# A four-layer graph network on one core: where the last blocks' own parts stand at the end of layer 1

## The chip, the cores and the metric

The kernel runs on one core of a Trainium2 chip. A core has TensorE (PE, matrix products), VectorE (DVE), ScalarE (ACT), GpSimd (POOL) and SyncE (SP). Each engine works through its own instructions in the order written and waits on semaphores for the others. POOL issues the gathers, SP nearly all other transfers. The metric is the device time of one launch in microseconds; lower is better.

## The reference, cut to what matters

Four graph layers run in turn on 3327 nodes with 512 features, each followed by a residual and a layer norm, all with the same 0/1 matrix `adj`:

```python
x = layernorm(x + L0_gat(x, adj))                 # attention, 8 heads of 64
x = layernorm(x + L1_mean(x, adj))                # relu(combine(self, mean of neighbours))
x = layernorm(x + L2_first64(x, adj))             # below
x = layernorm(x + L3_gat(x, adj))                 # attention, 4 heads of 128

# layer 2
keep = (A > 0) & (cumsum(A > 0, axis=1) <= 64)    # the first 64 neighbours of a row
nb_mean = keep @ X / max(keep.sum(axis=1), 1)
xj = leaky_relu(nb_mean @ W_nb.T + b_nb)          # zero where a row has no neighbours
xi = leaky_relu(X @ W_line.T + b_line)            # a node's "own part"
out = xi + xj
```

## The kernel before, in words

The nodes are cut into 26 blocks of 128 (the last, block 25, has 127). Every row of `adj` is first turned into lists of neighbours. Layers 1 and 2 then work block by block: a block has some chunks of 128 list places, a chunk's table rows are gathered from DRAM by an indirect DMA of POOL (L1018, `gather`), and TensorE multiplies a 0/1 selection matrix with the gathered rows and adds up in PSUM (L1879, `mean_group`). Layer 2's neighbour product is applied ahead of the gathering: the table `t2_d` holds `X @ W_nb.T + b_nb` for every node, in three bfloat16 pieces. A neighbour can be any node, so no gather of layer 2 can be issued before all 26 blocks are stored in `t2_d`.

The instruction order is written out by generators. A generator issues some instructions and yields; `work` holds groups of chunks, `ends` the tails of blocks, and one `step` lets every live generator go on to its next `yield`, in the order in which they were added. What is issued first stands first in its engine's queue. `both()` steps `work` and then `ends`.

The blocks come in the order `weave`: 1, 24, 23, ..., 9, 8, 7, 6, 25. After a block's sum is done, `layer1_end(b)` goes through these stages, one for each step:

- the layer's result with residual (L1933 to L1935) and the statistics (L811, L813), and a square root on ScalarE (L819);
- a reciprocal and three small corrections on VectorE (L821, L834 to L836), and the normalised block `xres[b]` (L851);
- its transposition on TensorE (L789), evacuated by ScalarE to `xt` (L792);
- the product with `wn2` (L806);
- the bias added into `tb` (L1946), and then, over the following steps, the split of `tb` into three pieces `t3` (L842 to L848, ScalarE and VectorE in turn), and the store into `t2_d` (L777, SP);
- three small products `acc0 += near0 @ t3` (L1958), which sum block 0's neighbours without a gather. Once all 26 are in, `acc0` is evacuated and added to `xres[0]` (L1963 to L1966).

The own part of layer 2, `own_part(b)`, needs only the normalised block: a product with `wl2` (L806) from the same `xt`, then three VectorE operations (L1977 to L1979) that add the result to `xres[b]`. For most blocks it is added to `ends` beside the split. For the last five blocks of `weave` (`LATE = 5`: 9, 8, 7, 6 and 25) it is put off: the block goes onto the list `late`, and its own part later transposes the block again. Before the change, block 9's own part is added when the last groups of layer 1 are under way, and the own parts of 8, 7, 6 and 25 after layer 2's first two groups of gathers have been issued.

Layer 2's stage opens after that. Its loads of `first2`, `raw3` and `a3` (L2037, L2043, L2046) go into space that `wn2` and `wl2` leave, so they wait for the last product with `wl2`. `score_weights` (L1570 to L1573) prepares layer 3's weights on VectorE, and `layer2_end(b)` is the tail of a block of layer 2. The gathers go into a ring of 19 chunks (tiles `gl` and `gk`). `select` (L1034) makes a selection matrix on VectorE and keeps it in `salla`, and later `sallb`.

Of the kernel before, what the change touches and what calls it, by code (L numbers as in the profile page):

```python
# [631 lines left out]
def sparse_path(ctx, tc, flag_i, x, adj, l0_w, l0_a1, l0_a2, l1_w_self, l1_b_self, l1_w_nb, l1_b_nb,  # L632
# [15 lines left out]
    NB = (N + P - 1) // P  # L648
# [7 lines left out]
    def row(src, n, rows=P):  # L656
        return bass.AP(tensor=src.tensor, offset=src.offset, ap=[[0, rows], [1, n]])

    def pool_in(lay, name, bufs=1, **kw):
        return lay.enter_context(tc.tile_pool(name=name, bufs=bufs, reuse_waits="tile", **kw))  # L660
# [23 lines left out]
    def mixed():  # L684


        left, ahead = list(range(1, NB - 1)), 0
        mean = sum(chunks_of[1:]) / (NB - 1)
        while left:
            b = left.pop(0 if ahead >= 0 else -1)  # L690
            ahead += mean - chunks_of[b]
            yield b
        yield NB - 1

    weave = list(mixed())
# [79 lines left out]
    def store(dst_d, b, t, shift=0):  # L775
        for p0, p1 in rows_of(b):
            nc.sync.dma_start(dst_d[shift + b * P + p0:shift + b * P + p1, :], t[p0:p1])  # L777
# [7 lines left out]
    def transposed(pool, ps, src, xsum=None, b=0):  # L785

        pt = ps.tile([P, DC, P], F32, name="pt", tag="tr")
        for c in range(DC):
            nc.tensor.transpose(pt[:, c, :], src[:, c * P:(c + 1) * P], ident)  # L789
        xt = pool.tile([P, DC, P], F32, name="xt")  # L790
        if xsum is None:
            nc.scalar.copy(xt, pt)  # L792
            return xt
        n = LAST if b == NB - 1 else P
        for c in range(DC):
            nc.scalar.activation(xt[:, c, :n], pt[:, c, :n], AF.Identity, accum_out=xsum[:, c, b:b + 1])  # L796
        if n < P:
            xs = pool.tile([P, DC], F32, name="xs")
            nc.vector.tensor_reduce(xs, xsum, AX.X, ALU.add)
            nc.vector.tensor_scalar(xt[:, :, n], xs, 1.0 / N, None, ALU.mult)  # L800
        return xt

    def times(ps, xt, w):
        po = ps.tile([P, D], F32, name="po")
        for c in range(DC):
            nc.tensor.matmul(po, xt[:, c, :], w[:, c], start=c == 0, stop=c == DC - 1)  # L806
        return po

    def moments(fin, y):
        st = fin.tile([P, 6], F32, name="st")  # L810
        nc.vector.bn_stats(st, y)  # L811
        mv = fin.tile([P, 2], F32, name="mv")
        nc.vector.bn_aggr(mv, st)  # L813
        return mv

    def root(fin, mv):

        r0 = fin.tile([P, 1], F32, name="r0")
        nc.scalar.activation(r0, mv[:, 1:2], AF.Sqrt, bias=eps)  # L819
        yield  # L820
        nc.vector.reciprocal(r0, r0)  # L821
        return newton(fin, mv, r0)
# [27 lines left out]
    def scaled(o, y, mv, rs):  # L850
        nc.vector.tensor_scalar(o, y, mv[:, 0:1], rs, ALU.subtract, ALU.mult)  # L851
# [1033 lines left out]
    ends = Stages()  # L1885

    def both():
        work.step()
        ends.step()
# [9 lines left out]
    with ExitStack() as lay:  # L1899
        fin = pool_in(lay, "l1f", 2)  # L1900
        wp = pool_in(lay, "l2b")
        bn = wp.tile([P, D], F32, name="bn")
        nc.sync.dma_start(bn, row(l2_b_nb, D))
        bl = wp.tile([P, D], F32, name="bl")
        nc.sync.dma_start(bl, row(l2_b_line, D))
        sp = pool_in(lay, "l1s", 3)
        ps = pool_in(lay, "l1ps", 2, space=PSUM)
        acc0 = pool_in(lay, "l1p0", space=PSUM).tile([P, D], F32, name="acc0")
        paccz = pool_in(lay, "l1pz", space=PSUM)
        nd = [0]  # L1910
        xts = pool_in(lay, "l1xt", 3)
        first = extra[:, 4 * D:].rearrange("p (s d) -> p s d", s=2)
        nc.sync.dma_start(first.bitcast(F32), t1_d[2:2 + P, :])
        early, late = list(range(NB - LATE0, NB - LATE0 + EARLY)), []

        def self_part(b):

            yield
            xt = transposed(xts, ps, xres[b])
            yield  # L1920
            zb = xin.get(b)
            if zb is None:
                zb = fin.tile([P, D], F32, name="tb")
            nc.scalar.copy(zb, times(ps, xt, wx))
            if b in xin:
                return
            store(z1_d, b, zb)

        def layer1_end(b, acc):
            yield  # L1930
            zb = xin.pop(b)
            y = fin.tile([P, D], F32, name="e")
            nc.vector.scalar_tensor_tensor(y, acc, rdeg[:, b:b + 1], zb, ALU.mult, ALU.add)  # L1933
            nc.vector.tensor_add(y, y, bias1)
            nc.vector.scalar_tensor_tensor(y, y, 0.0, xres[b], ALU.max, ALU.add)  # L1935
            mv = moments(fin, y)
            rs = yield from root(fin, mv)
            x2 = xres[b]
            scaled(x2, y, mv, rs)
            yield  # L1940
            xt = transposed(xts, ps, x2)
            yield
            po = times(ps, xt, wn2)
            yield
            tb = fin.tile([P, D], F32, name="tb")
            nc.vector.tensor_add(tb, po, bn)  # L1946
            t3 = fin.tile([P, 3, D], BF16, name="t3")
            if b not in weave[-LATE:]:
                ends.add(own_part(b, xt))
            else:  # L1950
                late.append(b)
            yield from pieces(t3, tb)
            store(t2_d, b, t3.rearrange("p s d -> p (s d)"), 2)
            yield
            m = LAST if b == NB - 1 else P
            nd[0] += 1
            for k in range(3):
                nc.tensor.matmul(acc0, near0[:m, b, :], t3[:m, k], start=nd[0] == 1 and k == 0,  # L1958
                                 stop=nd[0] == NB and k == 2)
            if nd[0] == NB:  # L1960
                yield
                y = fin.tile([P, D], F32, name="e")
                nc.scalar.mul(y, acc0, rnear)  # L1963
                yield
                nc.vector.scalar_tensor_tensor(y, y, SAGE_ALPHA, y, ALU.mult, ALU.max)
                nc.vector.tensor_add(xres[0], y, xres[0])  # L1966

        def own_part(b, xt=None):

            yield  # L1970
            if xt is None:
                xt = transposed(xts, ps, xres[b])
                yield
            po = times(ps, xt, wl2)
            yield
            xi = fin.tile([P, D], F32, name="xi")
            nc.vector.tensor_add(xi, po, bl)  # L1977
            nc.vector.scalar_tensor_tensor(xi, xi, SAGE_ALPHA, xi, ALU.mult, ALU.max)
            nc.vector.tensor_add(xres[b], xi, xres[b])  # L1979

        def made(b):

            xin[b] = fin.tile([P, D], F32, name="zb", bufs=3)
            if b < NB - LATE0 + EARLY:
                load(xin[b], z1_d, b)
            else:
                ends.add(self_part(b))

        for b in early:
            ends.add(self_part(b))  # L1990
        ends.drain()
        for item in woven(ring):
            b, at = item[0], item[4]
            if at == 0 and b or b == 0 and at + item[3] == NB:
                made(b)
            work.add(mean_group(item, t1_d, row0, lambda b, acc: ends.add(layer1_end(b, acc)), [first]))
            both()
            if b in weave[-HASTE:]:
                ends.step()
        ends.add(own_part(late.pop(0)))  # L2000
        while work.live:
            both()
        ends.drain()
        wxlay.close()
        rows = room.tile([P, RING], F32, name="gl", tag="ring")
        extra = aside.tile([P, MORE], F32, name="gk", tag="aside")
        ring = Ring(3 * D, rows.bitcast(BF16), extra.bitcast(BF16))
        sall = [(0, pool_in(ctx, "s_alla", side="right").tile([P, split, P], FP8, name="salla"))]
        nexts = groups(ring, weave, first=(1, 2))

        def second(b, acc):
            ends.add(layer2_end(b, acc))

        firsts = []
        for _ in range(2):
            work.add(mean_group(next(nexts), t2_d, None, second, firsts, sall))
            work.step()
        for b in late:
            ends.add(own_part(b))
        while ends.live:  # L2020
            ends.step()
    w2lay.close()


# [191 lines left out]
```

## Time and profile before

| | |
|---|---|
| median of 3 runs | 1661.63 us (1660.79 to 1669.61) |
| profiled execution | 1659.49 us, its span 1657.7 us |
| PE busy | 1487.2 us, 90% of the span |
| DVE busy | 1175.7 us, 71% |
| ACT busy | 903.4 us, 54% |
| POOL busy | 762.6 us, 46% |
| last gather of layer 1 issued | 1046.69 us |
| first gather of layer 2 issued | 1099.08 us |
| mean granted TensorE clock | 0.955 |

The first row is what the kernel is judged by. All other numbers are of one profiled execution, whose positions are counted from the start of its span. A row of instructions names the engine, the line of the kernel, the operation, what it writes and reads, and in brackets how long its engine had been idle and what ended that. Lines such as L789 and L806 are helpers that many places call, so the tile names tell which call it is: `po<-wn,xt` is a product for the table, `po<-wl,xt` one for an own part. The trace writes `wn2` as `wn` and `t2_d` as `t_d`, without numbers. One `times` call shows as eight product records, one `transposed` as four.

### The profile page before, as it was taken

The numbers are of one execution on the slowest core, as the hardware profiler recorded it, in microseconds if no ns is written. First come the engines' busy times: TensorE is split into PE (matmuls) and PEld (weight loads), VectorE is DVE, ScalarE is ACT, GpSimd is POOL, SyncE is SP. The second block draws the span as 40 slices with busy tenths as digits, with TensorE's granted clock in tenths as the row PEclk, the third lists the DMA queues.
The fourth block names the chain that finished last, engine by engine and source line by source line (L and its number), as shares of the span: only waits on it lengthen the run. The fifth ranks groups of instructions, "written<-read, shape, count | busy, mean of one in ns | idle before, by whom it ended". The sixth has DMA issues, their size and how long they took to land.

```text
span 1657.7 us, 24457 instructions
## 1 busy us (share of the span) xinstructions
PE 1487.2 (90%) x7305; PEld 998.9 (60%) x7341; DVE 1175.7 (71%) x3136; ACT 903.4 (54%) x3007; POOL 762.6 (46%) x994
## 2 busy tenths in 40 slices
PE   6789968999999999889999999887999996988885
PEld 4567746666666777435555555433566665777764
DVE  7998789998567789215566677648665644779886
ACT  5788865777667878412222121212344444679997
POOL 3000057665554520055444565137777702777770
PEclk9889979999999999879999999999999999999998
DMA  8877678876665542199788999348899812888881
GB/s 253 267 240 263 194 254 280 269 214 207 204 192 152 169 140 81 52 367 317 246 298 312 326 371 337 132 143 296 297 322 295 285 52 91 241 240 249 255 248 64
DMA packets 130402, 381.99 MB, mean 230 GB/s; under 512 B 22037, under 2 KB 36477, under 8 KB 130259
## 3 DMA queue, kind: packets, MB, share of 16 engines
q0 software_dynamic: 67696, 252.97, 47.6%
q1 hardware_dynamic: 62563, 127.35, 22.8%
q8 instruction: 60, 0.98, 0.2%
q14 instruction: 83, 0.68, 0.1%
HBM read 331.89 MB, written 48.37 MB: 229 GB/s over the span
## 4 chain that ended last, share of the span: by engine, by line
PE 63%; DVE 11%; ACT 9%; DMA 8%; issue 5%; POOL 3%; SPq 0%; ACTq 0%; DVEq 0%; POOLq 0%
PE po L806 19%; PE acc L1375 12%; PE po L1056 10%; PE acc L1879 9%; PE pt L789 3%; DMA gl<-t_d,idx 3%; DMA gt<-t_d,idx 1%; PE acc L1871 1%; PE acc L1263 1%; DVE gt L1356 1%; PE acct L1485 1%; DVE cand L909 1%; ACT m L882 1%; ACT upc L1412 1%; POOL gl L1018 1%
## 5 line engine op out<-in xcount | busy, mean ns | idle before, releaser
L1018 POOL DMA_INDIRECT gt<-t_d,idx x201 | 203.8, 1014 | 342.3 <-DVE eq L978 208.0
L1018 POOL DMA_INDIRECT gl<-t_d,idx x265 | 269.6, 1017 | 134.8 <-DMA t_d<-t 51.4
L1375 PE MATMUL acc<-gt,sel 128*128 128x264 f32 (+3 forms) x804 | 209.9, 408 | 4.4 <-DVE gt L1356 2.7
L1018 POOL DMA_INDIRECT gm<-t_d,idx x140 | 140.4, 1003 | 143.9 <-PE acc L1879 95.6
L806 PE MATMUL po<-wn,xt 128*128 128x512 f32 x416 | 193.9, 608 | 7.1 <-ACT h L1526 3.8
L1375 PEld LDWEIGHTS acc<-gt,sel 128*128 128x128 f32 (+3 forms) x804 | 153.4, 200 | 42.0 <-issue 13.9
L1375 PE MATMUL acc<-gl,sel 128*128 128x260 f32 (+3 forms) x524 | 137.5, 410 | 11.0 <-ACT r L1553 4.9
L806 PEld LDWEIGHTS po<-wn,xt 128*128 128x128 f32 x416 | 77.8, 194 | 89.1 <-issue 76.2
L1056 PE MATMUL po<-gt,xt 128*128 128x268 f32 x416 | 118.1, 428 | 14.1 <-ACT g0fall L1068 8.2
L1356 DVE TENSOR_TENSOR gt<-gt,pg 128x1536 f32<-128x1536 f32 (+3 forms) x64 | 116.6, 1822 | 13.6 <-ACT sel L1351 13.3
L792 ACT COPY xt<-pt 128x512 f32<-128x512 f32 x81 | 47.3, 588 | 130.8 <-PE pt L789 117.6
L1879 PE MATMUL acc<-gm,selr 128*128 128x512 f32 (+3 forms) x324 | 110.9, 462 | 7.3 <-DMA gm<-t_d,idx 5.0
L1375 PEld LDWEIGHTS acc<-gl,sel 128*128 128x128 f32 (+3 forms) x524 | 100.4, 201 | 27.1 <-ACT r L1553 5.2
L909 DVE MAX8 cand<-val 128x8 f32<-128x464 uint16 (+32 forms) x184 | 107.6, 620 | 0.1
L1056 PE MATMUL po<-w,xt 128*128 128x262 f32 x416 | 97.0, 386 | 8.0 <-ACT xt L796 5.1
L1018 POOL DMA_INDIRECT gk<-t_d,idx x65 | 65.7, 1011 | 82.3 <-DMA t_d<-mean 60.0
L1056 PEld LDWEIGHTS po<-gt,xt 128*128 128x128 f32 x416 | 79.2, 203 | 32.8 <-ACT g0fall L1068 8.6
L1308 ACT ACTIVATE far<-place,sites 128x128 int16<-128x128 int16 (+3 forms) x167 | 87.3, 543 | 13.1 <-DVE ds L1318 12.1
L806 PE MATMUL po<-wx,xt 128*128 128x512 f32 x208 | 93.6, 595 | 0.3 <-ACT vc L967 0.3
L789 PE MATMUL pt<-s_ident,xres 128*128 128x128 f32 x500 | 77.5, 283 | 17.7 <-POOL gt L1668 10.5
L806 PE MATMUL po<-wl,xt 128*128 128x512 f32 x208 | 93.1, 593 | 0.0
L1056 PEld LDWEIGHTS po<-w,xt 128*128 128x128 f32 x416 | 78.2, 190 | 24.0 <-ACT xt L796 9.8
(397 smaller groups left out, 3222.4 us busy)
## 6 DMA issues: line engine op xcount, KB each, us to landing
ab<-in_adj_dram SPq DMA_DIRECT2D x25, 832.0 KB
ab<-in_adj_dram SPq DMA_DIRECT2D x25, 831.5 KB
t_d<-t SPq DMA_DIRECT2D x25, 512.0 KB
gm<-t_d POOLq DMA_DIRECT2D x21, 512.0 KB
t_d<-t SPq DMA_DIRECT2D x25, 384.0 KB
t_d<-tg SPq DMA_DIRECT2D x25, 264.0 KB
gd<-t_d SPq DMA_DIRECT2D x25, 264.0 KB
t_d<-tg SPq DMA_DIRECT2D x25, 260.0 KB
```

The lines of the kernel that those rows point to most:

```text
L789: nc.tensor.transpose(pt[:, c, :], src[:, c * P:(c + 1) * P], ident)
L792: nc.scalar.copy(xt, pt)
L806: nc.tensor.matmul(po, xt[:, c, :], w[:, c], start=c == 0, stop=c == DC - 1)
L882: nc.scalar.activation(m[:, c0:], ab[s][:, c0:], AF.Sign, accum_out=half[:, s, b:b + 1])
L909: nc.vector.max(out=cand[:, s, :], in_=val[:, cuts[s]:cuts[s + 1]])
L1018: nc.gpsimd.indirect_dma_start(out=t[:m, c, :], out_offset=None, in_=table[:, :], in_offset=bass.IndirectOffsetOnAxis(ap=l.idx[:m, c0 + c: ...
L1056: nc.tensor.matmul(pw[s], xt[:, c, :], self.w[:, c, s, :], start=c == 0, stop=c == DC - 1)
L1263: nc.tensor.matmul(self.acc[h // hh][:, h % hh, :], wt[:m, h, :], G[:m, h, :], start=False, stop=False)
L1308: nc.scalar.activation(o, place[:, (c0 + q0) * P:(c0 + q1) * P], AF.Abs, bias=l.nmid[k], scale=2.0)
L1356: nc.vector.tensor_mul(Gc[:, :, :OUT], Gc[:, :, :OUT], w[:, :g].rearrange("p c (h o) -> p (c h) o", o=1).to_broadcast([P, g * H, OUT]))
L1375: nc.tensor.matmul(accs[b][s], S[:m, c, :], G[:m, c, s * hh * M:(s + 1) * hh * M], start=at + c == 0, stop=last)
L1879: nc.tensor.matmul(accs[b], chosen, parts[:, k * D:(k + 1) * D], start=at + c + k == 0, stop=k == top and at + c == n - 1)
```

## The change

Block 25's own part is now added to `ends` when its product for the table has been issued, with its `xt`, like that of an early block. In the same moment the own parts of the four blocks on `late` are added as two chains, 9 then 7 and 8 then 6. The early own part of block 9 goes. After that the steps go on only until block 25's three small products are issued (`nd` counts the blocks); then come layer 2's first two groups (gathers, and the first group's selection), and then what is left of `ends`: block 0's last operations and the own parts of 7 and 6.

```diff
             if b not in weave[-LATE:]:
                 ends.add(own_part(b, xt))
+            elif b != weave[-1]:
+                late.append(b)
             else:
-                late.append(b)
+                ends.add(own_part(b, xt))
+                for k in range(2):
+                    ends.add(own_parts(late[k::2]))
             yield from pieces(t3, tb)
             store(t2_d, b, t3.rearrange("p s d -> p (s d)"), 2)
             yield
...
+        def own_parts(bs):
+            for b in bs:
+                yield from own_part(b)
+
...
             both()
             if b in weave[-HASTE:]:
                 ends.step()
-        ends.add(own_part(late.pop(0)))
         while work.live:
             both()
-        ends.drain()
+        while nd[0] < NB:
+            ends.step()
         wxlay.close()
...
         for _ in range(2):
             work.add(mean_group(next(nexts), t2_d, None, second, firsts, sall))
             work.step()
-        for b in late:
-            ends.add(own_part(b))
-        while ends.live:
-            ends.step()
+        ends.drain()
```

## Prediction, made before the run

> **What bounds the kernel now.** I read the page first, then the chain of waits between 1040 and 1180 us, then the timeline there, then busy time by stretch. The page shows TensorE busy 90% of the span, but also one long idle stretch of POOL, the engine that issues the gathers:
>
> ```profile
> L1018 POOL DMA_INDIRECT gl<-t_d,idx x265 | 269.6, 1017 | 134.8 <-DMA t_d<-t 51.4
> ```
>
> The 51.4 us at the end of the line are one wait: after layer 1's last gather POOL waits for the last store into layer 2's table. Layer 2 can't gather before that, so the chain through block 25, the last of layer 1, sets its start. The timeline of that chain (start, duration, engine, line, operation; in brackets the idle time before it and what ended it):
>
> ```profile
> 1074.65 3.70 PE L806 MATMUL po<-wn,xt 128*128 128x512 f32 x8 [0.24 <-ACT xt L792]
> ...
> 1076.67 0.18 DVE L813 BATCH_NORM_AGGREGATE mv<-st 128x2 f32<-128x6 f32 x1
> 1078.39 0.69 DVE L1946 TENSOR_TENSOR tb<-po,bn 128x512 f32<-128x512 f32 x1 [1.53 <-PE po L806]
> 1081.82 0.69 DVE L1977 TENSOR_TENSOR xi<-po,bl 128x512 f32<-128x512 f32 x1 [2.74 <-PE po L806]
> 1082.54 0.69 DVE L1978 SCALAR_TENSOR_TENSOR xi<-xi 128x512 f32<-128x512 f32 x1
> 1083.27 0.69 DVE L1979 TENSOR_TENSOR xres<-xi,xres 128x512 f32<-128x512 f32 x1
> 1083.88 0.16 DVE L821 RECIPROCAL r<-r 128x1 f32<-128x1 f32 x1
> ...
> 1085.35 0.63 PE L789 MATMUL pt<-s_ident,xres 128*128 128x128 f32 x4 [2.92 <-DVE xres L851]
> 1086.71 5.14 PE L806 MATMUL po<-wn,xt 128*128 128x512 f32 x8 [0.73 <-ACT xt L792]
> ...
> 1091.89 0.69 DVE L1946 TENSOR_TENSOR tb<-po,bn 128x512 f32<-128x512 f32 x1 [3.99 <-PE po L806]
> ...
> 1099.08 0.95 POOL L1018 DMA_INDIRECT gl<-t_d,idx  x1 [51.37 <-DMA t_d<-t]
> ```
>
> The statistics of block 25 are there at 1076.85 and ScalarE's root of them at 1077.18 (1076.89 + 0.29). Yet the reciprocal that needs only these runs at 1083.88: it stands on VectorE behind the three operations of block 9's own part (L1977 to L1979), and the first of those waits for a product on TensorE. TensorE then finds nothing to do for 2.92 us, and the product for block 25 takes 5.14 us where the same product took 3.70 at 1074.65.
>
> What comes after the start, in stretches (length, busy us of PE, PEld, DVE, ACT, POOL, then granted clock, DMA share, GB/s):
>
> ```profile
> 1099.00:1120.00 21.00, 19.00 (x59) 8.23 (x59) 10.46 (x18) 1.87 (x2) 16.35 (x16) 1.00 0.82 258
> 1120.00:1140.00 20.00, 15.53 (x63) 5.88 (x63) 15.51 (x35) 3.38 (x11) 15.73 (x15) 1.00 0.93 331
> 1140.00:1160.00 20.00, 14.17 (x53) 6.15 (x53) 18.07 (x46) 5.14 (x21) 15.43 (x16) 0.83 0.84 264
> 1160.00:1180.00 20.00, 17.01 (x73) 8.20 (x74) 14.56 (x44) 5.20 (x18) 15.43 (x16) 1.00 0.90 289
> 1180.00:1200.00 20.00, 19.90 (x105) 13.74 (x106) 11.96 (x30) 9.85 (x52) 15.43 (x16) 1.00 0.89 297
> ```
>
> POOL issues gather after gather with 0.30 us between them, without a real wait, from 1099 to 1264; TensorE idles 13.3 us from 1120 to 1180 (60 less 15.53, 14.17 and 17.01) and is full from 1180. So the gathers lead, and TensorE's full stretch starts when they have fed it. An earlier first gather moves all of that.
>
> **What the Trainium skill says.** "TensorE: Matmul & The Clock Gate", What's actually happening: TensorE's clock halves after an idle window of about 3.4 us and needs a busy one to return; the window runs freely. Its section PE-mode transpose says that transposes don't count as busy in the same way. The trace agrees: no product runs from 1082.43 to 1086.71 (4.28 us), and the next has its first weight loads 0.85 us apart, then 0.43, at a mean clock of 0.72 (1086.7 to 1092). "DMA: Bandwidth & Descriptors", Two DMAs through the same engine are not ordered: the issuer must wait for the completion semaphore of what it reads. The trace agrees: the store issued at 1095.40 lands 2.45 us later, and POOL starts at 1099.08.
>
> **The change, part by part.**
>
> Removed ahead of block 25: block 9's own part, four transposes, an evacuation, a product and three VectorE operations. On VectorE the reciprocal can follow block 6's `tb`, which ends at 1079.08, in place of the last own operation, which ends at 1083.96 (1083.27 + 0.69). That is **4.88 us** earlier: reciprocal at 1079.00, `xres` done at 1080.33, transposes 1080.47, evacuation 1081.19, product 1081.83. What was hidden behind the own part is then late next: block 6's `tb` itself, which waits for TensorE until 1078.39; that bound is in the sum.
>
> The product: at full clock `tb` follows 3.74 us after its start (1078.39 − 1074.65), at the lowered clock 5.18 (1091.89 − 1086.71). In the new order TensorE has no product from about 1079.0 (block 7's three small ones end) to 1081.83: 2.8 us, with 0.63 of transposes. That is shorter than the window of the skill, so I take the full clock: `tb` at 1085.57, **6.32 us** earlier than 1091.89. At the lowered clock it is 1087.01, 4.88 earlier.
>
> From `tb` to the first gather are 7.19 us (1099.08 − 1091.89): casts and subtractions in turn, store, landing. Added inside it are the products of blocks 25, 9 and 8. Costed at nothing, because each stands behind the step it could delay in its engine's order: ScalarE's second cast (2.14 us after `tb`) is issued ahead of the evacuations of 9 and 8; VectorE's last subtraction (2.79) ahead of block 25's own three operations, whose product ends some 4.1 after `tb`. Block 25 needs no second transposition, since its `xt` is handed on, as that of the blocks ahead of the last five is. SP and POOL get no DMA more, and each keeps its order: store, then gathers. **First gather: 1092.8 instead of 1099.1.**
>
> The own parts behind it: before, the last product ends 20.0 us after `tb` (1111.93) and VectorE's last operation 22.2 after. New, counted from `tb`: block 6's small products 0.6, product of 25 3.45, two transpositions 1.1, products of 9 and 8 with their evacuation 7.1, block 25's small products 0.7, transpositions and evacuations of 7 and 6 1.5, their products 6.9: 21.3, and VectorE 23.5. So relative to the gathers it is 1.3 later (five own parts instead of four, one of them beside the casts), in absolute terms 5.0 earlier. Who waits: the selections of layer 2's second group on, TensorE's sums, and SP's loads of `first2`, `raw3` and `a3`, which wait for the weights' space. Cover: TensorE caught up at 1121.2 and then waited 0.80, 0.40, 0.27 and 0.32 us for gathers, so 1.3 are absorbed by the fourth; VectorE sat idle 3.43 us ahead of 1127.12, after `raw3` was used. If that cover is gone, the cost is at most 1.3.
>
> The reordered selection (0.28 us) and block 0's last three operations (some 2 us) cost nothing: nobody on the chain reads them, and the gathers ran on POOL, which they never held up. Bounds for both: minus 0.3 to plus 0.3.
>
> **Sum:** minus 6.3. On the profiled execution (1659.49; span 1657.7) that gives 1653.2; the median of the three runs, 1661.63, lies 2.1 above it, and on that I forecast **1655.3 us**.
>
> **Rivals.**
> The clock stays low. For it: at 1055 to 1057 TensorE was lowered although a 0.38 us product stood in the gap, and the window runs freely. Against it: the gap shrinks from 4.28 to 2.8. Then minus 4.9: 1656.8.
>
> The gain is partly handed back by layer 2's preparation, and, at the far end, more than that. `raw3` took 8.1 us from issue (1112.39) to use (1120.51) beside running gathers. It is now issued 1.3 later after the first gather. VectorE's 3.43 idle less 1.3 leaves 2.1; past a landing of 10.2 us the score weights (VectorE without pause from 1129.70 to 1141.58) move back against the gathers, `layer2_end` behind them too, and TensorE's hole of 4.79 us ahead of 1146.16 grows. A landing of 13 us would cost 2.8: 1658. **Slower** from a landing of 16.5 (10.2 + 6.3); at 20 us it gives 1665, at most one for one. For it: the DMA engines are 0.93 busy. Against it: the loads have their own queue and the load on DMA is the same as before.
>
> More than the sum: a shifted clock window also spares TensorE the lowered clock of 1140 to 1160 (20 us at 0.83 are 3.4 lost). Then 1652. Against it: TensorE isn't what leads there.
>
> That the change doesn't do what it says: the reciprocal would need another late input. None shows; its root was done at 1077.18.
>
> **How the numbers follow.** Full clock 0.57, low clock 0.22, partly handed back 0.08, slower 0.05, more than the sum 0.08. A difference of about 0.5% (8.3 us) is what a measurement of this kernel can tell from no change. The forecast lies inside it; it passes it only with the last case or a scatter of 2 us: faster 0.16. Slower by over 0.5% needs a landing beyond 25 us or a disturbed measurement: 0.04. Same: 0.80. The runs of before spread over 1 us and once 9; with that and the low-clock and handed-back cases the range is 1651.5 to 1660.0.
>
> **What would show it.** Right: no L1977 between the last two `tb` ahead of layer 2; the reciprocal straight after the first of them; the last product in 3.6 to 3.7 us; POOL's wait 45 us instead of 51.4; first gather at about 1092.8 and the gathers' pauses still 0.30; the last own operation near 1109. Wrong: a first gather later than 1095, or one at 1093 with TensorE's full stretch still starting at 1180.

## The result and the profile after

The changed kernel takes 1657.79 us (median of 13 runs, 1653.04 to 1663.97), the kernel before 1661.84 (13 runs, 1658.28 to 1669.61). The ratio, taken over runs on the same chip, is 0.9964 with a 95% interval of 0.9951 to 0.9978: 6.0 us faster (of 1661.84), within 3.7 to 8.1. The two medians lie only 4.05 apart, so the size is known no better than that interval. Forecast were 6.3 less, and 1655.3 us.

The page's row for POOL's gathers, with the wait ahead of layer 2 at its end, which was 51.4:

```profile
L1018 POOL DMA_INDIRECT gl<-t_d,idx x265 | 269.4, 1017 | 130.2 <-DMA t_d<-t 46.7
```

The timeline of the last blocks of layer 1 (start, duration, engine, line, operation, in brackets the idle time before it and what ended it):

```profile
1073.30 3.70 PE L806 MATMUL po<-wn,xt 128*128 128x512 f32 x8 [0.68 <-ACT xt L792]
...
1075.32 0.18 DVE L813 BATCH_NORM_AGGREGATE mv<-st 128x2 f32<-128x6 f32 x1
...
1077.04 0.69 DVE L1946 TENSOR_TENSOR tb<-po,bn 128x512 f32<-128x512 f32 x1 [1.53 <-PE po L806]
1077.64 0.15 DVE L821 RECIPROCAL r<-r 128x1 f32<-128x1 f32 x1
...
1079.11 0.63 PE L789 MATMUL pt<-s_ident,xres 128*128 128x128 f32 x4 [1.46 <-DVE xres L851]
...
1080.46 5.40 PE L806 MATMUL po<-wn,xt 128*128 128x512 f32 x8 [0.73 <-ACT xt L792]
...
1085.90 0.69 DVE L1946 TENSOR_TENSOR tb<-po,bn 128x512 f32<-128x512 f32 x1 [4.25 <-PE po L806]
...
1089.98 0.69 DVE L1981 TENSOR_TENSOR xi<-po,bl 128x512 f32<-128x512 f32 x1 [0.59 <-PE po L806]
...
1093.10 0.95 POOL L1018 DMA_INDIRECT gl<-t_d,idx  x1 [46.73 <-DMA t_d<-t]
```

The reciprocal (L821) now follows block 6's `tb` at once, and the first own part (`xi`, L1981) comes behind block 25's `tb`. Positions in two executions can't be subtracted as they stand: this one reached block 6's product 1.35 us earlier for reasons ahead of the change (1073.30 against 1074.65). So I count from there. The first gather came 24.43 us after the start of block 6's product before (1099.08 − 1074.65) and comes 19.80 after it now: 4.63 less, not 6.3, because block 25's product took 5.40 us here. That it stands at 1093.10, so near the 1092.8 of the forecast, is luck: the 1.35 earlier and the 1.7 of the slower product nearly cancel.

Whether the shift lasts shows at the first places where POOL, after some 170 us of gathers nearly all 0.30 us apart, has to wait for room in the ring again. From POOL's timeline of the kernel before, and then of the changed one:

```profile
1270.05 0.96 POOL L1018 DMA_INDIRECT gl<-t_d,idx  x1 [1.64 <-PE acc L1879]
```

```profile
1264.77 0.96 POOL L1018 DMA_INDIRECT gl<-t_d,idx  x1 [1.65 <-PE acc L1879]
```

The same wait of the same length comes 5.28 us earlier, 3.93 without the 1.35, and the last gather of layer 2 too (1319.94 against 1325.22). Yet the span shrinks by only 0.7 us, from 1657.7 to 1657.0. The place is TensorE's timeline at the end of layer 2, the product of its last block, before and after:

```profile
1387.82 3.77 PE L1056 MATMUL po<-w,xt 128*128 128x262 f32 x16 [2.85 <-DVE xt L800]
```

```profile
1382.53 6.74 PE L1056 MATMUL po<-w,xt 128*128 128x262 f32 x16 [2.85 <-DVE xt L800]
```

It follows the same pause of 2.85 us in both and took 3.0 us longer in this execution. The sum of the pair: 1.35 earlier ahead of the change, 4.63 gained by it, 0.70 handed back in layer 2, 3.01 lost to this product and its successors up to layer 3's first gather, 1.57 in layer 3. That is 0.7. One pair of executions would therefore have hidden the change; the runs don't.

### The profile page after: what moved, and what is told of

Its sections match the earlier page's. It is cut to its first block, busy times and chain, and to the rows that moved or that the text cites. A ratio compares the mean times of both kernels' runs of the same rounds, so it can differ in the third digit from the quotient of the medians.

```text
span 1657.0 us, 24451 instructions
## 1 busy us (share of the span) xinstructions
PE 1490.0 (90%) x7302; PEld 1001.0 (60%) x7337; DVE 1174.7 (71%) x3136; ACT 902.9 (54%) x3006; POOL 761.9 (46%) x994
## 4 chain that ended last, share of the span: by engine, by line
PE 64%; DVE 12%; ACT 8%; DMA 7%; issue 4%; POOL 4%; SPq 0%; DVEq 0%; ACTq 0%; POOLq 0%
PE po L806 20%; PE acc L1375 12%; PE po L1056 10%; PE acc L1879 10%; DMA gl<-t_d,idx 3%; PE pt L789 3%; POOL gl L1018 2%; PE acc L1263 2%; PE acc L1871 1%; DVE gt L1356 1%; DVE cand L909 1%; PE acct L1485 1%; PE acc L1962 1%; ACT m L882 1%; ACT upc L1412 1%
```

## The experiments

The first four experiments ran on one other chip, where the kernel before takes 1771.31 us (median of 75), and the two further profiles of the removal and of the changed kernel on a second one, where it took 1774.77 (one run). The rest ran where it takes 1662 to 1663. Only ratios, and distances inside one trace, are compared across chips.

**Only the removal.** The changed kernel's first part alone, in the kernel before:

```diff
-        ends.add(own_part(late.pop(0)))
         while work.live:
             both()
         ends.drain()
```

> Only the early own part of block 9 goes; the rest of the tail stays as before: the steps run to their end, layer 2's first two groups are issued, then five own parts (9, 8, 7, 6, 25), each with its own transposition. Theory (the gain is the 4.9 us that VectorE's queue held block 25's reciprocal, plus 1.4 where TensorE's clock stays up): counted from the start of block 6's table product, the first gather comes 19.8 us later, as in the changed kernel, against 24.4 before, and the time falls by 4 to 6 us against before. The own parts end some 4 us later after block 25's tb than before (24 instead of 20). Rival (the gain lies in the reordering, because own parts beside the casts free TensorE later): the own parts that all stand behind the first gathers now hold back layer 2's first sums by 4 us and the time stays within 2 us of before.

Measured: ratio 0.9966 (0.9947 to 0.9984), as large as the whole change. First gather 18.10 us after the start of block 6's product (1132.54 − 1114.44), where 19.8 was expected. The timeline from block 6's `tb` on:

```profile
1118.18 0.69 DVE L1946 TENSOR_TENSOR tb<-po,bn 128x512 f32<-128x512 f32 x1 [1.53 <-PE po L806]
1118.79 0.15 DVE L821 RECIPROCAL r<-r 128x1 f32<-128x1 f32 x1
...
1121.62 3.70 PE L806 MATMUL po<-wn,xt 128*128 128x512 f32 x8 [0.73 <-ACT xt L792]
...
1125.35 0.69 DVE L1946 TENSOR_TENSOR tb<-po,bn 128x512 f32<-128x512 f32 x1 [2.55 <-PE po L806]
...
1132.54 0.95 POOL L1018 DMA_INDIRECT gl<-t_d,idx  x1 [45.11 <-DMA t_d<-t]
1133.11 17.33 PE L806 MATMUL po<-wl,xt 128*128 128x512 f32 x40
```

Here the product ran at full clock, which the 19.8 did not assume, with the same order ahead of it as in the changed kernel. All five own-part products stand in one row behind the first gather and end 25.1 us after block 25's `tb`, VectorE's last own operation 27.3 after it (20.0 and 22.2 before the change). The time doesn't suffer. The rival, that the gain lies in the reordering, is refuted by the interval: it would leave the time within 2 us of before.

That later own parts cost nothing is shown only for this chip, and something there may hide their cost. ScalarE stops soon after layer 2's start (last section), and TensorE waits for it. Ahead of the same nine products TensorE stood idle 7.88 us in the removal, and 14.88 in the changed kernel, whose own parts end sooner (profile of its third run, below):

```profile
1180.45 3.90 PE L1879 MATMUL acc<-gl,salla 128*128 128x512 bf16 x9 [7.88 <-issue]
```

```profile
1175.36 3.86 PE L1879 MATMUL acc<-gl,salla 128*128 128x512 bf16 x9 [14.88 <-ACT e L2076]
```

The removal alone was not run where the kernel before takes 1662 to 1663 us; the traces there show no such stop.

**Only the reordering.** The changed kernel with `ends.add(own_part(late.pop(0)))` put back ahead of the loop:

> The reordering alone: block 9's own part stays ahead of block 25, the own parts of 25, 8, 7, 6 come behind block 25's table product and the first gathers are issued ahead of their rest. Theory: from the start of block 6's table product to the first gather 24.4 us as before, own parts done 3 us earlier after tb than before, no gain in time: within 2 us of before. Rival (the reordering gains): 3 us or more faster than before.

Measured: ratio 1.0006 (0.9990 to 1.0022), and the first gather 24.38 us after block 6's product starts (1136.28 − 1111.90), as before, with POOL's wait as long as before:

```profile
1136.28 0.95 POOL L1018 DMA_INDIRECT gl<-t_d,idx  x1 [51.30 <-DMA t_d<-t]
```

The last own operation ends 20.1 us after `tb` instead of 22.2: 2.1 earlier, not 3, and worth nothing that the runs can tell.

**The pause filled.** The changed kernel, in `layer1_end` for block 25:

```diff
             scaled(x2, y, mv, rs)
+            if b == weave[-1]:
+                idle = ps.tile([P, D], F32, name="po")
+                for c in range(2):
+                    nc.tensor.matmul(idle, ident, wl2[:, c], start=c == 0, stop=c == 1)
             yield
             xt = transposed(xts, ps, x2)
+            if b == weave[-1]:
+                nc.tensor.matmul(idle, ident, wl2[:, 2], start=True, stop=True)
```

> The changed kernel with three products of the identity with a column block of wl2 put into TensorE's pause ahead of block 25's table product (two ahead of its transposition, one behind it; their sums go to a PSUM buffer that nobody reads). Theory (the product takes 5.4 us because the pause lets the clock fall): the product takes 3.6 to 3.8 us again, its start is 0.2 to 0.5 later, and the first gather is 1.1 to 1.5 us earlier than in the changed kernel, counted from the start of block 6's table product (18.4 to 18.7 instead of 19.8); time 1 us below the changed kernel. Rival (the product is slow for another reason, such as its operands): still 5.1 to 5.4, and the first gather 0.3 later.

Measured: the product took 3.70 us and the first gather came after 18.17 us (1126.24 − 1108.07); ratio 0.9964 (0.9946 to 0.9982). The duration is as the clock theory has it, but one profile proves little, since the same kernel without fillers shows 3.70 too (below). The expected gain of 1 us is beneath what the interval can tell.

**Block 25 held up.** The changed kernel with

```diff
-            scaled(x2, y, mv, rs)
+            for _ in range(25 if b == weave[-1] else 1):
+                scaled(x2, y, mv, rs)
```

> The changed kernel in which block 25's normalisation (one VectorE operation of 0.55 us) is written 25 times instead of once, so that only its chain gets longer. Theory (layer 2 runs at the gathers' pace and what follows moves with the first gather, one for one): first gather some 14 us later, time 13 to 15 us above the changed kernel, about 8 to 9 above before. Rival (TensorE, full from 1180 on, takes up part of the shift): less than 10 us above the changed kernel.

Measured: ratio 1.0053 (1.0035 to 1.0071) to before, which is 1.0053 / 0.9964 = 1.0089 to the changed kernel, 15.8 us of 1771, with some 4 us of doubt either way. The first gather came 34.09 us after block 6's product (1149.14 − 1115.05), 14.3 to 16.0 later than the 19.80 and 18.10 seen without the delay:

```profile
1149.14 0.94 POOL L1018 DMA_INDIRECT gl<-t_d,idx  x1 [60.64 <-DMA t_d<-t]
```

So a later first gather costs about its full length, and the rival's less than 10 us is refuted by the interval. From layer 2's first to its last gather it is 252.15 us here and 253.5 to 255.1 in the three others of this series, so these profiles leave room for TensorE's full stretch to take up 1 to 3 us of the delay.

**The changed kernel again,** for a second profile:

> The changed kernel as it is, for a second profile beside the next two. Theory (whether block 25's table product runs at full clock is a matter of where the clock's window falls): from the start of block 6's table product to the first gather either 18.1 us (product 3.7) or 19.8 (product 5.4); time 0.3 to 0.4% below before. Rival (the order of the changed kernel always lets the clock fall, and the order with all own parts behind the gathers does not): 5.4 again.

Measured: ratio 0.9966 (0.9951 to 0.9980), block 25's product again 5.40 us, first gather again after 19.81. That spoke for the rival, so both kernels were run once more, side by side. **The removal again:**

> The kernel of e1 once more, for its profile. Up to block 25's table product it issues the same instructions in the same order as the changed kernel. Theory (the product's duration depends on where the pause of 2.8 us falls in the clock's window, not on the order of instructions): product 3.7 or 5.4, and not bound to this kernel. Rival (this kernel's order keeps the clock up): 3.7 again, beside 5.4 in the changed kernel.

**And the changed kernel a third time:**

> The changed kernel once more, for its profile, on the same chip as the run of e1's kernel beside it. Theory: 3.7 or 5.4, as there. Rival: 5.4 a third time, with 3.7 beside it.

TensorE's timeline of the removal alone, and then of the changed kernel, from block 6's product to block 25's:

```profile
1105.75 3.70 PE L806 MATMUL po<-wn,xt 128*128 128x512 f32 x8 [0.67 <-ACT xt L792]
...
1109.29 0.81 PE L1958 MATMUL acc<-t,near 128*128 128x512 bf16 x3
...
1111.56 0.63 PE L789 MATMUL pt<-s_ident,xres 128*128 128x128 f32 x4 [1.47 <-DVE xres L851]
...
1112.92 5.25 PE L806 MATMUL po<-wn,xt 128*128 128x512 f32 x8 [0.73 <-ACT xt L792]
```

```profile
1110.81 3.70 PE L806 MATMUL po<-wn,xt 128*128 128x512 f32 x8 [0.67 <-ACT xt L792]
...
1114.34 0.81 PE L1962 MATMUL acc<-t,near 128*128 128x512 bf16 x3
...
1116.62 0.63 PE L789 MATMUL pt<-s_ident,xres 128*128 128x128 f32 x4 [1.46 <-DVE xres L851]
...
1117.98 3.70 PE L806 MATMUL po<-wn,xt 128*128 128x512 f32 x8 [0.73 <-ACT xt L792]
```

The roles are exchanged. Same instructions, pauses within 0.01 us, and each of the two kernels has now shown both durations. The order does not decide it. First gathers: after 19.66 and 18.08 us. Single times, 1762.59 and 1765.42 beside 1774.77 for before, tell no more than that.

**One more step of the same kind.** The changed kernel with the newest block stepping first until block 25's product is issued:

```diff
+        ends.newest = True
         while work.live:
             both()
...
             else:
+                ends.newest = False
                 ends.add(own_part(b, xt))
```

> The changed kernel with one more step of the same kind: while layer 1's last groups and the steps up to block 25's table product are issued, the newest block steps first, so that block 25's reciprocal stands ahead of block 6's tb on VectorE. Theory (after the own part, that tb is what the reciprocal waits for): reciprocal 1.8 us earlier after the start of block 6's product, block 25's product 1.3 earlier and at full clock, since TensorE's pause shrinks below 1 us; first gather 16.8 us after the start of block 6's product; time 1.3 to 3 us below the changed kernel, 0.45 to 0.55% below before. Rival (block 6's delayed split, whose last piece now stands behind block 25's tb, holds the store and so the gathers): first gather no earlier than 18.1.

Measured: 1652.13 us, ratio 0.9947 (0.9928 to 0.9966) to before; the changed kernel beside it had 1657.40. The timeline, from block 6's product on:

```profile
1070.98 3.70 PE L806 MATMUL po<-wn,xt 128*128 128x512 f32 x8 [0.68 <-ACT xt L792]
...
1073.00 0.18 DVE L813 BATCH_NORM_AGGREGATE mv<-st 128x2 f32<-128x6 f32 x1
...
1073.69 0.15 DVE L821 RECIPROCAL r<-r 128x1 f32<-128x1 f32 x1
...
1074.93 0.68 DVE L1946 TENSOR_TENSOR tb<-po,bn 128x512 f32<-128x512 f32 x1
...
1076.85 3.70 PE L806 MATMUL po<-wn,xt 128*128 128x512 f32 x8 [1.06 <-ACT xt L792]
...
1087.80 0.95 POOL L1018 DMA_INDIRECT gl<-t_d,idx  x1 [43.49 <-DMA t_d<-t]
```

The reciprocal no longer waits for block 6's `tb`; the first gather comes 16.82 us after the start, as expected. Against the changed kernel that is 1.3 to 3.0 us less, and block 6's product itself starts 0.4 us sooner after block 7's (11.29 us against 11.70). The medians of this series differ by 5.3, and all six times, up to 1655.79, lie below the changed kernel's median; the further gain is likely, but its size isn't settled.

**The other pause filled as well.** In `layer2_end`, for the last block, behind its transposition:

```diff
+            if b == NB - 1:
+                idle = ps.tile([P, w3.shape[3]], F32, name="po")
+                for c in range(5):
+                    nc.tensor.matmul(idle, ident, w3[:, c % DC, 0, :], start=c == 0, stop=c == 4)
```

> The kernel with the newest block first, and besides five products of the identity with layer 3's weights (their sum goes to a PSUM buffer that nobody reads) in TensorE's pause ahead of layer 2's last block's product, where 3.77, 5.46 and 6.74 us have been seen for the same product. Theory (the clock's window again): that product takes 3.8 us, and layer 3's first gather comes 1.7 to 3 us earlier after layer 2's last gather than where it was slow (73.6 on this kind of chip), time 1 to 2 us below the kernel without them. Rival (the fillers delay the product they are to speed up): no gain.

Measured: the last block's product took 3.77 us. From layer 2's last gather to layer 3's first it was 72.38 us (1389.46 − 1317.08), against 74.17 without the fillers (1386.89 − 1312.72), 1.8 less. The time was 1652.43 us, ratio 0.9946 (0.9928 to 0.9964): no gain that the runs can tell. Two slips in the expectation: the 73.6 in it is a distance on the slower chips, and the product's 3.8 is no proof by itself, since 3.77 occurs without fillers as well.

## Why the prediction was right

**Which wait led.** Right. Taking the own part out from ahead of block 25 brings the first gather forward and earns the whole gain (on one chip 0.9966 alone, 1.0006 for the reordering alone, and 0.9964 for both with the fillers; 0.9964 for the change on the chip of the result).

**The 4.88 us on VectorE.** Right to a tenth: where the product ran at full clock, the first gather came 18.10 and 18.08 us after block 6's product, where the steps give 24.43 − 6.32 = 18.11. At the lowered clock they give 24.43 − 4.88 = 19.55, and 19.80, 19.81 and 19.66 were seen. What the prediction named as late next, block 6's `tb`, was next: ordered behind the reciprocal, it gave up another 1.3.

**The product at full clock.** In the profiled execution of the result this step failed: the product took 5.40 us, as in the rival at 0.22. It stood on weaker ground than its chance of 0.57 said. I put the pause of 2.8 us beside the window of about 3.4 in the Trainium skill ("TensorE: Matmul & The Clock Gate", What's actually happening) and took it as short enough. In five profiles with this pause the product took 5.40, 5.40 and 5.25 us, and twice 3.70. The traces show that the lowered clock makes the difference: over the product the mean granted clock was 0.68, 0.68 and 0.70 in the slow three and 1.00 in the other two. In each of the slow three it stood at 0.50 for some 3.4 us, in the result's profile from 1081.4 to 1084.8.

The fall came 0.9 and 0.4 us after the product's start in two of them and 0.3 ahead of it in the third (5.25 us); in the fast two there was none in the pause or the product. That it isn't tied to an instruction fits the page's remark that the window runs freely. But a pause of 2.8 us can't hold a whole idle window of 3.4, wherever that falls. So the page's rule, as I used it, and its advice to keep gaps below some 3 us (Why this matters for your kernels), don't protect here. Where the pause was filled or shortened, all three profiles show 3.70; since two with the pause do too, that the pause lets the clock fall is supported, not shown.

**The steps after `tb`.** Right: 7.20 us to the first gather (1093.10 − 1085.90) where 7.19 were taken from before; VectorE's last own operation 23.5 after `tb`, as worked out. The handing back that the cover was to prevent didn't come in the changed kernel: `raw3` was used 7.2 us after its issue (8.1 before). For own parts that end later still, as in the removal alone (27.3 after `tb`), the cost stays open, as said there. Two readings of the prediction are a little off, without bearing on the sum: the 2.45 us of the store count from 1095.77, not from its issue at 1095.40, and the waits of 0.80, 0.40 and 0.27 us already make up the 1.3, so that the third absorbs them.

**One for one.** Right as far as it can be told: layer 2's first to last gather took 226.14 us before and 226.84 after, and a delay of 14 to 16 us cost 15.8, give or take 4. The sign of being wrong, TensorE's full stretch still starting at 1180, didn't show: TensorE was busy 16.68 us from 1154 to 1174 and 19.95 from 1174 to 1194. Nor did the case of more than the sum: from 1134 to 1154 the clock was 0.83, as in the same stretch before.

**The size.** 6.0 measured against 6.3. With the lowered clock in part of the executions the sum would have been 4.9 to 6.3, and 4.6 to 6.3 by the first gathers seen; the interval holds all of these. That the two figures agree to 0.3 is in part luck: both profiles of the changed kernel on the chips that run it in 1658 us show the lowered clock, and with it a first gather only 4.6 us earlier.

## What to carry to other kernels

At the end of a stage, find the last block's chain and list what stands ahead of it in each engine's queue without being needed by it: here three operations of a neighbour, waiting for a product, held the chain to the next layer up by 4.9 us, while the same work moved behind the first gathers showed no cost in the times, though a stop on that chip may have hidden one. A pause of TensorE in such a chain may be charged twice, as itself and as a slower product after it. A single profile then can't judge a change of a few microseconds: count from a common instruction, and leave the verdict to repeated runs.

## What the runs showed of the hardware

The product of layer 2's last block, always after the same pause of 2.85 us, took one of three durations without fillers: 3.8, 5.5 or 6.8 us (3.77 in three profiles, 5.46 in five, 6.74 and 6.80 in two of the changed kernel). The stretch from layer 2's last gather to layer 3's first follows it on each chip: 72.43, 74.17 and 75.44 us on the one. The granted clock explains the steps: it stood at 0.50 for 6.8 us around the product of 6.74 (1381.7 to 1388.6), for 3.4 us in that of 5.46 with the newest block first (1376.7 to 1380.1), and at no time during those of 3.77.

The two other chips ran the kernel before 6.6% and 6.8% slower (1771.31 and 1774.77 us against 1661.84). In all six profiles there ScalarE stops once for 15.6 to 28.3 us early in layer 2, ahead of an operation on a block's sum, and the profile shows nothing in the kernel that ends the stop. In the five profiles of the faster runs the longest idle time ahead of this operation is 6.3 us. In the changed kernel the stop looks so:

```profile
1174.62 0.69 ACT L2076 ACTIVATE e<-acc,rdeg 128x512 f32<-128x512 f32 x1 [23.24 <-issue]
```

What it is stays open. The removal alone gained there about what the whole change gained on the chip of the result (0.9966 and 0.9964).
